# Block attention of a Perceiver layer: neighbours' tiles loaded by one repeating transfer, rotation on VectorE, sums over keys in halves

## The chip, the cores and the metric

The kernel runs on one core of a Trainium2 chip. The metric is the device time of one execution in microseconds. The kernel before took 2400.67 us (median of 3 runs, 2400.48 to 2401.24).

## The reference

x is (16, 64, 256), that is 1024 rows of 256; the context ctx_2048 is (16, 1601, 256). The layer adds three blocks to x, each on a layer-normalised x:

1. Cross attention with weights and activations rounded to 8 bits: self-attention over the 64 rows of a sequence, and attention of the 64 rows over the 1601 context rows (16 heads of 128 in 8 groups of keys), then a projection. It is nearly all of the work.
2. Block attention with ternary weights, the block that the change touches:

```python
qkv = bitlinear(rmsnorm(x, attn_norm_w), qkv_w).reshape(B, S, 3, NH, HD)   # 16 heads of 16
q = apply_rope(q, cos, sin)
k = apply_rope(k, cos, sin)
qb, kb, vb = (blk(q), blk(k), blk(v))        # blocks of bt = S // 8 = 8 rows
scores = jnp.einsum('bnhqd,bnhkd->bnhqk', qb, kb) * HD ** (-0.5)
scores = jnp.where(causal, jnp.finfo(scores.dtype).min, scores)
attn = jax.nn.softmax(scores, axis=-1)
ctx = jnp.einsum('bnhqk,bnhkd->bnhqd', attn, vb)
x1 = x + bitlinear(ctx, o_w)
hn = rmsnorm(x1, ffn_norm_w)
gate, val = jnp.split(hn @ ffn_up_w.T, 2, axis=-1)
return x1 + bitlinear(jax.nn.silu(gate) * val, ffn_down_w)
```

   Here x is (16, 64, 256), so S = 64: each row attends only to the rows of its own block of 8, up to itself. apply_rope turns each pair of halves (x1, x2) of a head into x1 cos - x2 sin, x2 cos + x1 sin. bitlinear rounds its input to 8 bits, row by row, by the row's largest absolute value, and multiplies by weights in -1, 0, 1.
3. A gated feed-forward network with ternary weights, 256 to 704 to 256, with scales by row.

## The kernel before

**Tiles and order.** The 1024 rows are NT = 8 tiles of 128 rows (two sequences each), which stay on the chip as xr[i]. The cross attention of a tile is cut into four units (half of the heads, one sequence), each of 13 chunks of 128 context rows; a step is one chunk, and a tile takes 52 steps. For each chunk a unit projects keys (ps_k, L624), stores them in DRAM (kd, L655), reads them back transposed (kT, L665), multiplies them with the queries (s, L696), and later, 18 to 20 steps on, subtracts the maximum (L754), takes the exponential (L758) and accumulates with the context rows ctxN (acc, L772). The 13 chunks of several units are in flight at once, so the engines always have the next chunk's work.

All parts of the kernel are written as Python generators, put into a heap with a step and a rank, with hand-written lists of the steps between the pieces (SCHEDULE, PACE). The heap gives one recorded order of instructions. The framework's scheduler then orders the instructions of each engine from that, and its pools give out the buffers, so a change in one place can move instructions of all engines. At run time each engine's queue, SP's and ACT's queues of transfers too, is worked off strictly in order. Transfers take eight semaphore lanes in turn, so that an issue may have to wait for the eighth before it.

**The changed part.** `last_parts(i, start)` (L990) does blocks 2 and 3 for tile i, spread over the steps of later tiles' cross attention. For the last tile nothing is left beside it except chunks of the feed-forward network of tiles 3 to 6 (LATE, L1209), which `fill(...)` places among its parts: `gated` (L1173: product pgu_late on TensorE, tanh on ACT, sg_late and hd_late on VectorE) and `down` (L1196: po_f, ot, output). Its steps:

- Normalise, quantise (`act_quant`, L961), multiply by the ternary weights: qk (128 rows x 512: 16 heads of 16 for q, then the same for k) and v (128 x 256).
- Rotate: GpSimd (POOL) writes r1 = qk times the cosines (L1018), VectorE writes r2 = the swapped halves times the sines in two instructions (L1024) and adds r2 to r1 (L1029).
- Store the rotated k and v in DRAM as kv, e = 0 for k and e = 1 for v, each as two halves a = 0, 1 of 8 heads, 128 rows x 128 (L1034).
- `near(e, a)` (L1037) loads, for every row, the 8 rows of its block side by side: a tile of 128 x 1024 floats in which row p holds the 8 x 128 values of block p // 8. That is the same 16 x 1024 floats eight times over. Eight transfers of 64 KB do it, the k-th one writing rows k, 8 + k, 16 + k and so on. They are issued on SP; for K of the last tile every other one goes on ACT's queue. So 32 transfers a tile: K a=0, K a=1, later V a=0, V a=1.
- `product(out, x, y, order)` (L1046) multiplies on VectorE over the whole 128 x 1024 (L1049) and sums by one reduction (L1050). For the scores it multiplies the row's q, repeated over 8 neighbours, with K and sums over the 16 channels. For the result cx it multiplies the softmax with V and sums over the 8 neighbours, for which the reduction reads with a stride.
- Mask, maximum, exponential and division between the two (L1065 to L1076).
- cx is quantised by `act_quant`: am (L965) is the row's largest absolute value, aq_q (L974) the rounded values, tr_aq their transposition on TensorE (L982); then po_o (L1093), xa, another norm, and the rest of the block.

`near` and `prod` tiles come from the pool wp (tag "w", 10 buffers), from which the weights' pieces (wproj, wup, w_ff, w_dn, tern_w) come as well. Tile i's last_parts run during the cross attention of tiles i+1 and i+2; those of the last one end the kernel.

Of the kernel before, what the change touches and what calls it, by code (L numbers as in the profile page):

```python
# [19 lines left out]
ALU = mybir.AluOpType  # L20
AX = mybir.AxisListType
PSUM = bass.MemoryType.PSUM

P = 128
# [49 lines left out]
def body(tc, ctx, a):  # L74
    nc = tc.nc
    V, A, PE, GP = nc.vector, nc.scalar, nc.tensor, nc.gpsimd
# [763 lines left out]
    def fill(where):  # L840
        n = FILL.get(where, 0)
        for fn in late[:n]:
            fn()
        del late[:n]
# [100 lines left out]
    def b2(name):  # L945
        return one.tile([P, 512], F32, tag="b2", name=name, bufs=3)

    def rmsnorm(src, wrow, name):
        sq = b1("sq3")
        ss = small.tile([P, 1], F32, tag="ss3", name="ss3")  # L950
        A.activation(sq, src, AF.Square, accum_out=ss)
        ms = small.tile([P, 1], F32, tag="ms1", name="ms1")
        V.tensor_scalar(ms, ss, 1.0 / H, EPS, ALU.mult, ALU.add)
        rs = small.tile([P, 1], F32, tag="rs1", name="rs1")
        GP.tensor_tensor(rs, ms, nhalf[:, 0:1], ALU.pow)
        yield 1
        h = b1(name)
        V.scalar_tensor_tensor(h, src, rs, wrow, ALU.mult, ALU.mult)
        return h
# [30 lines left out]
    def last_parts(i, start):  # L990
        need(8, "x", i)
        last = i == NT - 1
# [6 lines left out]
        h = yield from rmsnorm(xa, rows[:, 0, :], "h")  # L999
# [15 lines left out]
        if last:  # L1015
            fill("rope")
        r1, r2 = b2("r1"), b2("r2")
        GP.tensor_tensor(  # L1018
            r1.rearrange("p (h d) -> p h d", h=32), qk.rearrange("p (h d) -> p h d", h=32),
            rope[:, 0:16].unsqueeze(1).to_broadcast([P, 32, 16]), ALU.mult,  # L1020
        )
# [10 lines left out]
        kv = dram.tile([2, 2, P, P], F32, tag="kv3", name="kv3")  # L1032
# [3 lines left out]

        def near(e, a):  # L1037
            t = wp.tile([P, 1024], F32, tag="w", name="near")
            src = kv[e, a].rearrange("(n j) c -> n (j c)", j=8)
            for k in range(8):  # L1040

                q = nc.scalar if last and e == 0 and k % 2 else nc.sync
                q.dma_start(out=t.rearrange("(n t) x -> n t x", t=8)[:, k, :], in_=src)
            return t

        def product(out, x, y, order):  # L1046

            t = wp.tile([P, 1024], F32, tag="w", name="prod")
            V.tensor_tensor(t.rearrange("p (h j d) -> p h j d", h=8, j=8), x, y, ALU.mult)  # L1049
            V.reduce_sum(out, t.rearrange("p (h j d) -> p " + order, h=8, j=8), axis=AX.X)  # L1050

        near_k = [near(0, a) for a in range(2)]
        yield 2
        sc = one.tile([P, 16, 8], F32, tag="sc3", name="sc3")
        for a in range(2):
            if last:
                fill("sc%d" % a)
            product(
                sc[:, 8 * a : 8 * a + 8, :],
                r1[:, a * P : (a + 1) * P].rearrange("p (h d) -> p h d", h=8).unsqueeze(2).to_broadcast([P, 8, 8, 16]),  # L1060
                near_k[a].rearrange("p (j h d) -> p h j d", j=8, h=8), "h j d",
            )
            yield 1
        near_v = [near(1, a) for a in range(2)]
        V.tensor_tensor(sc, sc, cmask.unsqueeze(1).to_broadcast([P, 16, 8]), ALU.add)  # L1065
        mx = small.tile([P, 16], F32, tag="mx3", name="mx3", bufs=2)
# [11 lines left out]
        cx = one.tile([P, H], F32, tag="cx3", name="cx3")  # L1078
        for a in range(2):
            if last:  # L1080
                fill("av%d" % a)
            product(
                cx[:, a * P : (a + 1) * P].rearrange("p (h d) -> p h d", h=8),
                sc[:, 8 * a : 8 * a + 8, :].unsqueeze(3).to_broadcast([P, 8, 8, 16]),
                near_v[a].rearrange("p (j h d) -> p h j d", j=8, h=8), "h d j",
            )
            yield 1
        to = ternary_piece(1536, 512).rearrange("p (k o) -> p k o", k=2)
# [176 lines left out]
    for i in range(NT):  # L1265
        base = 52 * i
        for hh in range(2):
            for bb in range(2):
                unit(i, hh, bb, base + 26 * hh + 13 * bb)
            spawn(base + 26 * hh + 13 + 34 - 2 + (2, 1)[hh], 6.5, paced("pair", pair_out(i, hh, 4 if i < NT - 1 or hh == 0 else None)))  # L1270
        ln0, sa0, qx0 = SCHEDULE[i] if i in SCHEDULE else (
            base - 22, [base + o for o in (-15, 0, 8, 21)], [base + o for o in (-16, -7, 15, 18)]
        )
        spawn(ln0, 1.0, paced("ln" if i else "ln_first", ln_tile(i)))
        for p in range(4):
            spawn(sa0[p] - 2, 5.0, paced("sa", self_attention(i, p)))
            spawn(qx0[p] - 2, 3.0, paced("qx", queries(i, p)))
        l0 = base + {NT - 3: 95, NT - 2: 88, NT - 1: 82}.get(i, 90)
        spawn(l0, 4.5, paced("last" if i < NT - 1 else "last_tile", last_parts(i, l0)))
    spawn(-8, 1, bias_rows())  # L1280
    spawn(60, 5.7, ternary())
    order = [(kind, p) for p in range(4) for kind in ("wq", "wkv", "wqx", "wproj")]
# [76 lines left out]
```

## Time and profile before

| | us |
|---|---|
| median of 3 runs | 2400.67 (2400.48 to 2401.24) |
| the profiled execution | 2402.98 |
| its span, first to last instruction | 2400.8 |
| mean granted TensorE clock | 0.991 |
| ACT busy | 1667.5 |
| instructions in all | 40267 |
| transfers near<-kv | 248 on SP, 8 on ACT, 64 KB each |
| bytes moved | 485.17 MB, 202 GB/s on average |

The profile is of one execution. Engines are PE (TensorE), PEld (its weight loads), DVE (VectorE), ACT (ScalarE), POOL (GpSimd) and SP, and L12 is line 12 of the kernel. A row of a timeline has the start in us from the beginning of the span, the busy time, the engine and line, the operation, the output and inputs by the program's names, their shapes, how often it stands there in a row, and in brackets the idle time before it with what ended it. In rows of stretches come start:end, its length, the busy time of PE, PEld, DVE, ACT and POOL with the number of instructions, the granted clock, the share of the DMA engines' time and GB/s. In the line of 40 slices each digit is the busy share of 60 us in tenths.

For the changed lines the groups of the profile give: L1049 1.22 us, L1050 1.21 us for the scores and 1.86 to 1.93 for cx, L1029 0.69, L1018 (POOL) 1.27 to 1.51, L1024 0.41 to 1.50, one near issue on SP 0.587 in the median.

### The profile page before, as it was taken

To read this page: it belongs to the slowest core of one execution; us is meant where nothing else is said; L and a number is where in the kernel's file an instruction comes from. 1 tells how busy PE (TensorE), PEld (TensorE's weight loads), DVE (VectorE), ACT (ScalarE), POOL (GpSimd) and SP (SyncE) were. 2 spreads that over 40 slices of the span, in tenths; PEclk is the share of its full clock that TensorE was granted. 3 is DMA by queue.
4 is the path that set the end of the run, shared out by engine and by line. 5 is a ranking of instruction groups with operands and counts; after the bars stand their busy time and mean duration, and the time that the engine had idled before them with its cause. 6 is when DMAs were issued, how large, how long until landed. Compare 5 with 4: busy or idle time off the path is not lost.

```text
span 2400.8 us, 40267 instructions
## 1 busy us (share of the span) xinstructions
PE 2319.9 (97%) x12477; PEld 1761.5 (73%) x12477; DVE 1856.3 (77%) x4562; ACT 1667.5 (69%) x3744; POOL 798.4 (33%) x1016
## 2 busy tenths in 40 slices
PE   7999999999999999999999999999999999999995
PEld 4567777777777777877777777777777777677874
DVE  7577777878887788778887879777888777876766
ACT  4667777776876777767776777777677777776631
POOL 3333223333232433334333333324334343242200
PEclk9999999999999999999999999999999999999998
DMA  8889878876977779776987779877697776965323
GB/s 257 240 236 248 244 180 222 208 195 170 272 216 190 183 204 256 200 208 164 240 233 191 205 184 241 223 191 187 174 261 214 193 174 176 272 172 141 115 92 111
DMA packets 683661, 485.17 MB, mean 202 GB/s; under 512 B 464476, under 2 KB 592952, under 8 KB 683448
## 3 DMA queue, kind: packets, MB, share of 16 engines
q1 hardware_dynamic: 682904, 481.91, 75.4%
q8 instruction: 100, 1.64, 0.3%
q14 instruction: 113, 0.93, 0.1%
q10 hardware_dynamic: 544, 0.69, 0.1%
HBM read 271.03 MB, written 113.11 MB: 160 GB/s over the span
## 4 chain that ended last, share of the span: by engine, by line
PE 70%; DVE 11%; issue 5%; DMA 5%; ACT 4%; POOL 4%; SPq 1%; ACTq 0%; POOLq 0%; DVEq 0%
PE acc L772 22%; PE ps_k L624 21%; PE s L696 12%; PE po_x L863 2%; PE po_p L329 2%; ACT P L706 2%; PE ps_q L378 2%; POOL rsx L568 2%; POOL rs L223 1%; DMA kT<-kd 1%; DVE P L754 1%; PE sc L490 1%; PE pgu L1180 1%; PE tr_pc L799 1%; DVE M L715 1%
## 5 line engine op out<-in xcount | busy, mean ns | idle before, releaser
L772 PEld LDWEIGHTS acc<-ctxN,P 128*128 128x128 f32 (+1 forms) x4160 | 713.3, 191 | 212.3 <-issue 135.2
L772 PE MATMUL acc<-ctxN,P 128*128 128x257 f32 (+5 forms) x4160 | 799.8, 338 | 4.8 <-DMA ctxN<-in_ctx_n 2.7
L624 PE MATMUL ps_k<-wkx,ctxT 128*128 128x512 f32 x1600 | 760.2, 597 | 12.5 <-DVE wkx L1252 9.4
L706 ACT ACTIVATE P<-s,rsx 128x128 f32<-128x128 f32 x1536 | 439.4, 373 | 136.5 <-PE s L696 131.7
L567 POOL TENSOR_SCALAR vx<-ss 128x4 f32<-128x4 f32 x402 | 140.0, 348 | 1112.7 <-DVE ss L564 742.2
L568 POOL TENSOR_TENSOR rsx<-vx,nhalf 128x4 f32<-128x4 f32 x402 | 457.0, 1137 | 33.0
L624 PEld LDWEIGHTS ps_k<-wkx,ctxT 128*128 128x128 f32 x1600 | 278.1, 192 | 210.4 <-issue 189.9
L696 PE MATMUL s<-qx,kT 128*128 128x128 f32 x3072 | 412.1, 277 | 9.1 <-ACT qn L388 3.2
L696 PEld LDWEIGHTS s<-qx,kT 128*128 128x128 f32 x3072 | 377.6, 192 | 25.9 <-ACT qn L388 4.7
L715 DVE TENSOR_TENSOR M<-P,M 128x512 f32<-128x512 f32 (+1 forms) x384 | 263.6, 686 | 154.2 <-ACT P L706 138.3
L651 ACT COPY kh<-ps_k 128x1024 uint16<-128x1024 uint16 x360 | 366.6, 1018 | 4.9 <-DMA kd<-kh 4.9
L758 ACT ACTIVATE P<-P 128x512 f32<-128x512 f32 (+1 forms) x416 | 266.3, 641 | 141.4 <-DVE P L754 139.3
L559 ACT ACTIVATE sq<-ps_k 128x512 f32<-128x512 f32 x402 | 243.0, 604 | 167.8 <-PE ps_k L624 131.0
L564 DVE TENSOR_REDUCE ss<-sq 128x4 f32<-128x512 f32 x402 | 272.9, 679 | 27.2 <-ACT sq L559 27.0
L754 DVE TENSOR_TENSOR P<-P,mx 128x512 f32<-128x512 f32 (+1 forms) x416 | 284.0, 683 | 0.0
L223 POOL TENSOR_TENSOR rs<-ve,nhalf 128x4 f32<-128x4 f32 (+2 forms) x128 | 126.1, 986 | 287.6 <-DVE ve L222 267.8
L229 DVE TENSOR_SCALAR qn<-qn,mv,rs 128x128 f32<-128x128 f32 x256 | 76.8, 346 | 46.0 <-POOL rs L223 45.1
L219 DVE BATCH_NORM_STATS2 st<-qn 128x6 f32<-128x128 f32 x256 | 64.7, 273 | 23.4 <-ACT qn L388 23.4
L306 ACT CAST w_hi<-wproj 128x1024 fp32r<-128x1024 f32 x60 | 63.3, 1056 | 27.2 <-DMA wproj<-wproj 23.7
L307 DVE TENSOR_TENSOR wproj<-wproj,w_hi 128x1024 fp32r<-128x1024 f32 x60 | 73.0, 1219 | 9.4 <-ACT w_hi L306 8.7
L417 POOL TENSOR_TENSOR q_y<-qn,brow 128x512 f32<-128x512 f32 x32 | 51.8, 1619 | 53.4 <-DVE qn L229 45.9
L329 PE MATMUL po_p<-wproj,cat 128*128 128x256 f32 x272 | 67.0, 293 | 0.0
(233 smaller groups left out, 2817.9 us busy)
## 6 DMA issues: line engine op xcount, KB each, us to landing
kd<-kh SPq DMA_DIRECT2D x375, 256.0 KB
ctxT<-in_ctx SPq DMA_DIRECT2D x192, 256.0 KB
ctxN<-in_ctx_n SPq DMA_DIRECT2D x384, 128.0 KB
wproj<-wproj SPq DMA_DIRECT2D x68, 512.0 KB
wq<-wq SPq DMA_DIRECT2D x32, 512.0 KB
wkv<-wkv SPq DMA_DIRECT2D x32, 512.0 KB
wqx<-wqx SPq DMA_DIRECT2D x32, 512.0 KB
near<-kv SPq DMA_DIRECT2D x248, 64.0 KB
```

Source lines behind the costliest of these rows:

```text
L223: GP.tensor_tensor(rs[:, :g], ve[:, :g], nhalf[:, :g], ALU.pow)
L559: A.activation(sq[:n], ps[:n], AF.Square)
L564: ordered("dve", V.reduce_sum(ss[:n], sq[:n].rearrange("p (g d) -> p g d", g=4), axis=AX.X))
L568: ordered("pool", GP.tensor_tensor(rs[:n], ve[:n], nhalf[:n, 0:4], ALU.pow))
L624: PE.matmul(ps[:n, :], lhsT=st["cxT"][c // 2][:, k, o : o + n], rhs=wkx[:, k, 512 * hh : 512 * (hh + 1)], start=k == 0, stop=k == 1,)
L651: A.copy(t, src.bitcast(U16).rearrange("p (c e) -> p e c", e=2))
L696: PE.matmul(ps[:n, g * P : (g + 1) * P], lhsT=kT[:, g, 0:n], rhs=qxs[i, hh][:, bb, 2 * g : 2 * g + 2, :].rearrange("p h s -> p (h s)"), st ...
L706: A.activation(pc[:, g * P : (g + 1) * P], ps[:, g * P : (g + 1) * P], AF.Copy, scale=rs[:, g : g + 1])
L715: ordered("dve", V.tensor_tensor(st["M"][:n], pc[:n], st["M"][:n], ALU.max))
L754: ordered("dve", V.tensor_tensor(pc[:n], pc[:n], st["mx"][:n].rearrange("p g q -> p (g q)"), ALU.add))
L758: A.activation(pc[:n], pc[:n], AF.Exp)
L772: m = PE.matmul(ps, lhsT=pc[:n, g * P : (g + 1) * P], rhs=cx[:n, o : o + w], start=g < 3 and c == 0, stop=c == NC - 1, skip_group_check=g ...
```

## The change

Three edits, all in `last_parts`. The cosine product of the rotation is computed on VectorE instead of GpSimd. `near` issues one transfer of 512 KB per tile, whose source repeats each block's 1024 floats eight times (a stride of zero in the middle of 16 x 8 x 1024), all on SP but K a=1 of the last tile, which goes on ACT. `product` returns the products; the scores are reduced as before, and cx is summed by three additions in place: 8 neighbours to 4 (512 values of each row), 4 to 2 (256), 2 to 1 (128).

```diff
         r1, r2 = b2("r1"), b2("r2")
-        GP.tensor_tensor(
+        V.tensor_tensor(
             r1.rearrange("p (h d) -> p h d", h=32), qk.rearrange("p (h d) -> p h d", h=32),
             rope[:, 0:16].unsqueeze(1).to_broadcast([P, 32, 16]), ALU.mult,
         )
...
         def near(e, a):
             t = wp.tile([P, 1024], F32, tag="w", name="near")
-            src = kv[e, a].rearrange("(n j) c -> n (j c)", j=8)
-            for k in range(8):
-
-                q = nc.scalar if last and e == 0 and k % 2 else nc.sync
-                q.dma_start(out=t.rearrange("(n t) x -> n t x", t=8)[:, k, :], in_=src)
+            q = nc.scalar if last and e == 0 and a else nc.sync
+            q.dma_start(
+                out=t, in_=kv[e, a].rearrange("(n j) c -> n (j c)", j=8).unsqueeze(1).to_broadcast([16, 8, 1024])
+            )
             return t
 
-        def product(out, x, y, order):
+        def product(x, y):
 
             t = wp.tile([P, 1024], F32, tag="w", name="prod")
             V.tensor_tensor(t.rearrange("p (h j d) -> p h j d", h=8, j=8), x, y, ALU.mult)
-            V.reduce_sum(out, t.rearrange("p (h j d) -> p " + order, h=8, j=8), axis=AX.X)
+            return t
...
-            product(
-                sc[:, 8 * a : 8 * a + 8, :],
+            t = product(
                 r1[:, a * P : (a + 1) * P].rearrange("p (h d) -> p h d", h=8).unsqueeze(2).to_broadcast([P, 8, 8, 16]),
-                near_k[a].rearrange("p (j h d) -> p h j d", j=8, h=8), "h j d",
+                near_k[a].rearrange("p (j h d) -> p h j d", j=8, h=8),
+            )
+            V.reduce_sum(
+                sc[:, 8 * a : 8 * a + 8, :], t.rearrange("p (h j d) -> p h j d", h=8, j=8), axis=AX.X
             )
...
-            product(
-                cx[:, a * P : (a + 1) * P].rearrange("p (h d) -> p h d", h=8),
+            t = product(
                 sc[:, 8 * a : 8 * a + 8, :].unsqueeze(3).to_broadcast([P, 8, 8, 16]),
-                near_v[a].rearrange("p (j h d) -> p h j d", j=8, h=8), "h d j",
+                near_v[a].rearrange("p (j h d) -> p h j d", j=8, h=8),
+            ).rearrange("p (h x) -> p h x", h=8)
+            for n in (64, 32):
+                V.tensor_tensor(t[:, :, 0:n], t[:, :, 0:n], t[:, :, n : 2 * n], ALU.add)
+            V.tensor_tensor(
+                cx[:, a * P : (a + 1) * P].rearrange("p (h d) -> p h d", h=8), t[:, :, 0:16], t[:, :, 16:32], ALU.add
             )
```

## The prediction

> **What bounds the kernel now.** I read the busy shares and slices first, then busy time by stretch, then the timelines of the queues in the stretches that lose time.
>
> ```profile
> PE 2319.9 (97%) x12477; PEld 1761.5 (73%) x12477; DVE 1856.3 (77%) x4562; ACT 1667.5 (69%) x3744; POOL 798.4 (33%) x1016
> PE   7999999999999999999999999999999999999995
> PEclk9999999999999999999999999999999999999998
> ```
>
> TensorE is the bound: busy for 2319.9 of 2400.8 us at nearly full clock. No VectorE instruction saved in the middle is worth its own length; only idle time of PE can be won. The changed code runs once for each of eight tiles of rows, the first about 500 us in, the last in the final 55 us. The second view is busy time by stretch (start:end, length, then PE).
>
> ```profile
> 580.00:605.00 25.00, 23.36 (x129) 18.14 (x129) 21.89 (x50) 17.01 (x38) 9.63 (x11) 1.00 0.69 174
> 1153.00:1178.00 25.00, 24.34 (x130) 18.27 (x129) 22.68 (x52) 17.59 (x37) 9.61 (x11) 1.00 0.77 189
> 2025.00:2060.00 35.00, 32.60 (x161) 22.48 (x160) 30.09 (x72) 24.72 (x55) 10.14 (x13) 1.00 0.89 226
> 2270.00:2290.00 20.00, 15.21 (x82) 12.84 (x81) 18.01 (x39) 9.81 (x19) 0.93 (x1) 0.91 0.62 201
> 2340.00:2370.00 30.00, 11.99 (x54) 7.99 (x51) 21.94 (x40) 3.60 (x8) 1.51 (x1) 0.73 0.50 147
> ```
>
> The first three are what follows the loading of V's neighbours in three tiles: PE misses 1.64, 0.66 and 2.40 us. The stretches 867:892, 1438:1463 and 1718:1743 miss 0.97, 1.27 and 1.29 (24.03, 23.73, 23.71 of 25), so the six make 8.2 us. Quiet ones lose nothing (1000:1025 and K's 823:848 have 25.00 of 25). All of 520:2270 has 1729.67 of 1750: 20.3 idle. 2270:2290 loses 4.8, and 2340:2370 loses 18, which is the tail: the last tile's chain with too little else to do.
>
> Why PE misses time after V's transfers is in SP's timeline and in PE's rows just behind it:
>
> ```profile
> 1153.12 9.96 SPq L1043 DMA_DIRECT2D near<-kv  x16
> 1163.13 0.58 SPq L688 DMA_DIRECT2D qb<-qbd  x1
> 1163.81 1.68 SPq L665 DMA_TRANSPOSE kT<-kd  x1
> 599.96 0.46 PE L772 MATMUL acc<-ctxN,P 128*128 128x257 f32 x1 [1.38 <-DMA ctxN<-in_ctx_n]
> 1173.35 0.46 PE L696 MATMUL s<-qx,kT 128*128 128x128 f32 x2 [0.29 <-DMA kT<-kd]
> ```
>
> Sixteen issues hold SP for 10 us (0.6 each); the loads behind them (kT, ctxN) are late for PE some 10 us on. The tail is read on VectorE, SP, ACT and PE:
>
> ```profile
> 2342.47 1.84 DVE L1024 TENSOR_TENSOR r<-qk,shp 128x256 f32<-128x256 f32 x2 [0.66 <-ACT qk L1006]
> 2347.01 15.19 SPq L1043 DMA_DIRECT2D near<-kv  x24
> 2346.98 5.44 ACTq L1043 DMA_DIRECT2D near<-kv  x8
> 2351.61 1.23 DVE L1049 TENSOR_TENSOR prod<-r,near 128x1024 f32<-128x1024 f32 x1 [4.82 <-DMA near<-kv]
> 2361.95 1.86 DVE L1050 TENSOR_REDUCE cx<-prod 128x128 f32<-128x1024 f32 x1
> 2364.30 1.23 DVE L1049 TENSOR_TENSOR prod<-sc,near 128x1024 f32<-128x1024 f32 x1 [0.49 <-DMA out<-ot]
> 2367.45 0.42 DVE L965 TENSOR_REDUCE am<-cx 128x1 f32<-128x256 f32 x1
> 2369.55 0.39 PE L982 MATMUL tr_aq<-identb,aq_q 128*128 128x128 bf16 x2 [13.13 <-DVE aq_q L974]
> ```
>
> VectorE waits 4.8 us for K's neighbours, then works through to am at 2367.45, and PE waits 13.1 us for that. What moves am moves the end.
>
> **Tail, part by part.** *Rotation.* Beside POOL's product VectorE's two take 1.84 us. On VectorE alone: one 128x512 and two 128x256 products, which follow one another at 0.61 and 0.34 (intervals of such rows): 1.29 plus the interleaved late chunk. The sum of r1 starts some 0.3 us earlier (0 to 0.6), and with it the store of r.
> *K.* Before, the first of two K tiles lands at 2351.61, 4.6 us after its first issue. After: two transfers of 512 KB, on SP and ACT, issued about 2346.7; first packets 0.9 to 1.0 later, as now; 1 MB at 290 to 366 GB/s (366 is what the queue moved at 2366–2372; now it moves 105 to 172 here) is 2.9 to 3.6 us; 0.5 to the wake-up. Both land at about 2351.1 (2349.7 to 2352.6). SP then issues the late output row and both V; another 1 MB behind K, at 2351 + 3.6, is there at about 2355, and is needed only after two K products, two sums and the softmax (4.9 + 2.3), at 2358. ACT is no longer held for 5.44 us, so the late chunks' tanh, which came 7.4 us late at 2352.47, moves into the wait for K.
> *VectorE's chain.* From the first product to am it takes 15.84 us now. Out of it go: late chunks at 2354.01–2355.46, 1.45 (into K's wait); two ot rows, 0.66; the wait for V, 0.49; two cx sums of 1.89, replaced by adds on 512, 256 and 128 elements, 0.72 + 0.46 + 0.32 = 1.50 when each waits for the one before, so 0.78. Left: 12.5 (11.6 if other work fills the gaps between dependent ones, by intervals 0.61, 0.34, 0.21; 12.7 with all steps dependent). am then comes at 2351.1 + 12.5 = 2363.6 rather than 2367.45: **3.9 us** (2352.6 + 12.7 gives 2.1; 2349.7 + 11.6 gives 6.2). Behind am nothing changes, PE's clock is at 0.50 there already, and wup, issued at 2363.34 now, is issued earlier, since SP loses 28 issues.
>
> **Body.** *SP.* Per tile 32 issues become 4: 28 x 0.6 = 17 us of SP time gone. K's were spread over 25 us at no loss; V's cost the 8.2 us above. In tile seven, 2270:2290 loses 4.8: PE waits 4.06 at 2284.94 for an aq_q whose am is at 2280.40 behind the second cx at 2277.98; in the changed order of VectorE this cx comes some 20 instructions earlier. At best 8.2 + 4.8 = 13.0; at worst nothing is won and the new order loses as much elsewhere. The changed order of instructions differs from about 500 us on, on every engine (PE differs in 7115 lines), and the 25 us idle in 520:2290 is an average of what such orders lose. I take half: **6.5**.
> *VectorE.* Per tile 0.95 (the rotation row of 1.37 against 0.42 beside POOL) goes and 0.61 comes; sums save 0.8 to 1.5. Hidden: 77% busy, and PE is the bound. If that cover were gone, 1.5 x 7 = 10 us more gain.
> *New waits on VectorE.* Between the rotation's last sum and the first K product stand 23 VectorE instructions rather than 52 in tiles one to five, 14 and 7 in tiles six and seven; by their row lengths 11.9 us (26.7 before), 7.5 and 4.5. K needs, from tile three's rows (sum 1103.10, store 1104.49, first near 1108.69) and a landing of 5.84 us as for a 512 KB wproj in the chain of waits: 11.4 us, or 9 if SP comes sooner. Tiles one to five are covered (VectorE is not always busy, so 11.9 lasts 13 or so); tiles six and seven may stop VectorE for 2 and 4 us. Queued behind are P and M products that PE needs; PE can run on for about as long. I take **-1** (0 to -6).
> *POOL.* One instruction of 1.27 to 1.5 us a tile goes; POOL is at 33%, worth 0.
>
> **A rule against it.** The trace first: VectorE's second rotation row takes 1.37 us while POOL's L1018 runs and 0.42 otherwise, but P's products (L754, two operands in SBUF, mean 684 ns) and M's (686 ns) show no lengthening although POOL runs its small power (L568, 1.04 us x402) a third of the time. The Trainium skill, page "SBUF — State Buffer", section "Who interferes with whom", says that a VectorE instruction with two SBUF inputs and a GpSimd one reading SBUF exclude each other, and that reductions do not contend. By it the adds in halves are exposed where the sums were not: 48 adds at a third of the time by half of 1.04 is 8 us of VectorE; by the rows 0. The measured rows decide; in the tail POOL has no row from 2344 to 2372.
>
> **Sum.** 3.9 + 6.5 - 1 = 9.4. The profiled execution took 2402.98 us (span 2400.8), 2.3 above the median of the runs, 2400.67; the difference goes on the median: **2391.3 us**.
>
> **Rivals.** *Only the tail* (0.16): the new order loses as much as SP wins; for it: the idle 8.2 is what one fixed order leaves late, and another order can be late at another load; against: quiet stretches lose nothing. 2400.67 - 3.9 = 2396.8.
> *SP parked on V* (0.15, the slower side): V a=1 waits in each of tiles one to six for a buffer that VectorE frees, directly behind V a=0, and the next in SP's queue is the transpose of kT that PE reads. In the changed order K's second product stands 15 us of VectorE work behind the first, and V close to it. For a hold of W us, by the rate above (10 us cost 1.4): -3.9 - 8.2 + 6 x (1.4 + W - 10); it decides from W = 10.6, and W = 14 gives 2400.67 + 20 = 2421. Against: before, V's first issue waits for VectorE too, and SP reached it without pause at 1153.12.
> *The repeat isn't spread* (0.04): if one DMA engine carried a whole transfer, 128 rows x 0.2 us (4 KB packets take 0.17 to 0.27) = 26 us; K and V in the tail would cost about 40 and tiles more: 2440 and above. Against: its destination is 128 rows and each row one 4 KB run, as now.
> *No change* (0.03): order and tail cancel, 2400.
>
> **How the numbers follow.** Likeliest case 0.62, own range 2381.5 (6.2 + 13.0) to 2397. What is no change for this kernel: within 0.2%, 4.8 us. Only-the-tail (2.1 to 6.2) is faster by more in about 0.06 of its 0.16, else the same. Faster 0.68, same 0.13, slower 0.19. The range 2381.5 to 2401 holds the first two cases and no change; the slower ones are left out.
>
> **What would show it.** SP: four near issues a tile of about 0.6 us, none followed by a pause in SP above 10 us before the next kT. PE: the six stretches after V at most 0.5 us idle each, tile seven's wait for tr_aq under 2 us. Tail: K landing near 2351 less the body's gain, am 12.5 us after the first product, adds at 0.69, 0.42 and 0.28. Wrong if a K landing takes over 8 us, VectorE waits for near in tiles one to five, or the cx adds are slower than 1.9 us together.

## The result and the profile after

The changed kernel takes 2409.28 us (median of 10 runs, 2405.61 to 2416.88), the kernel before beside it 2400.95 (2396.88 to 2404.91). The ratio is 1.0037, 95% interval 1.0027 to 1.0048: slower by some 9 us, where 9.4 us less was forecast. The profiled execution has a span of 2408.0 us.

The tail did what was forecast, nearly. From the last tile's qk on ACT (L1006; 2341.75 before, 2352.19 after) to the end of the span it takes 55.8 us instead of 59.05. So 3.2 us are won there, and the body before it ends 10.4 us later. Busy time by stretch of the changed kernel shows where (PE is the column after the length, the last three are granted clock, DMA share and GB/s):

```profile
580.00:600.00 20.00, 16.00 (x76) 12.10 (x75) 11.28 (x32) 10.26 (x22) 6.41 (x9) 0.83 0.87 242
872.00:892.00 20.00, 16.09 (x93) 12.31 (x92) 11.82 (x31) 12.86 (x26) 7.14 (x11) 1.00 0.99 276
1160.00:1180.00 20.00, 15.33 (x79) 12.27 (x78) 11.56 (x33) 10.27 (x20) 6.54 (x10) 0.83 0.91 266
2270.00:2290.00 20.00, 20.00 (x135) 17.72 (x134) 11.18 (x20) 12.01 (x30) 2.66 (x4) 1.00 0.26 83
520.00:2270.00 1750.00, 1716.29 (x9346) 1316.90 (x9353) 1367.84 (x3360) 1274.14 (x2850) 584.37 (x750) 0.99 0.77 202
```

Tile seven's stretch, which lost 4.8 us before, loses nothing. But 520:2270 has 33.7 us without PE instead of 20.3, and 23.0 of them lie in six stretches of 20 us, one behind each of tiles one to six: the three shown and 1450:1470, 1735:1755 and 2015:2035 (15.20, 16.76 and 17.59 busy). Outside the six, 10.7 us are idle: the places that lost time before have been emptied (the 145 us behind V's issues of tiles one to six have PE busy for 144.03), and one new place has been opened in each of these tiles.

What happens there is in the chain of waits of tile three (start, duration, what) and in the view of who waited for whom (total, times, longest):

```profile
1164.97 0.46 SPq L255
...
1166.40 5.56 DMA wq<-wq
...
1171.99 1.05 ACT w_hi L306
...
1173.07 0.04 DVE wq L307
...
1174.21 0.69 DVE red L723
...
1175.04 0.37 PE tr_r L438
```

```profile
ACT w_hi L306 <- DMA wq<-wq: 19.5, 11, 3.4
DVE wq L307 <- ACT w_hi L306: 20.9, 9, 4.0
PE tr_r L438 <- DVE red L723: 21.1, 7, 4.8
```

wq is a piece of self-attention's weights (512 KB, L298), of another part of the kernel. It is loaded into the same pool wp as near and prod. ACT casts it to w_hi (L306), VectorE subtracts that from it (L307). red is a maximum over keys that VectorE takes for the cross attention (L723), and tr_r its transposition on TensorE (L438). In the changed kernel SP issues the second wq piece of a tile at 1166.40, behind the two wup loads (L255), and it lands 5.56 us later; ACT comes to the cast 3.0 us before that and holds everything behind it; VectorE is held at L307, its reduction red (L723) behind that is late, and PE waits 4.67 us at tr_r. None of these instructions is in the diff. The issue, the cast and tr_r in the timelines of the changed kernel:

```profile
1166.40 0.38 SPq L298 DMA_DIRECT2D wq<-wq  x1
1171.99 1.04 ACT L306 CAST w_hi<-wq 128x1024 fp32r<-128x1024 f32 x1 [3.00 <-DMA wq<-wq]
1175.04 0.37 PE L438 MATMUL tr_r<-ident,red 128*4 128x128 f32 x1 [4.67 <-DVE red L723]
```

In the kernel before the same wq is cast 7.0 us behind its issue, with no wait, and the view of waits has only the third of these rows:

```profile
1183.23 0.69 SPq L298 DMA_DIRECT2D wq<-wq  x1
1190.23 1.04 ACT L306 CAST w_hi<-wq 128x1024 fp32r<-128x1024 f32 x1
PE tr_r L438 <- DVE red L723: 0.3, 1, 0.3
```

It is the same in the other tiles. ACT comes to the cast of the second wq piece 7.0 to 7.8 us behind its issue in tiles one to five of the kernel before (3.4 in tile six, with a wait of 0.55); in tiles one to six of the changed kernel it comes 2.1 to 4.5 us behind it, and can begin after 5.4 to 7.3.

The tail after, in the timelines of SP, ACT, VectorE and PE:

```profile
2357.22 0.53 SPq L1040 DMA_DIRECT2D near<-kv  x1
2357.15 0.61 ACTq L1040 DMA_DIRECT2D near<-kv  x1
2361.85 1.23 DVE L1048 TENSOR_TENSOR prod<-r,near 128x1024 f32<-128x1024 f32 x1 [1.42 <-DMA near<-kv]
2364.13 1.23 DVE L1048 TENSOR_TENSOR prod<-r,near 128x1024 f32<-128x1024 f32 x1 [1.06 <-DMA near<-kv]
2374.57 0.42 DVE L965 TENSOR_REDUCE am<-cx 128x1 f32<-128x256 f32 x1
2376.66 0.40 PE L982 MATMUL tr_aq<-identb,aq_q 128*128 128x128 bf16 x2 [17.75 <-DVE aq_q L974]
```

From qk to am it is 22.38 us (2352.19 to 2374.57), 25.70 before.

### The profile page after: what moved, and what is told of

It reads as the page before. It is cut to its first block, busy times and chain, and to the rows that moved or that the text cites. A ratio compares the mean times of both kernels' runs of the same rounds, so it can differ in the third digit from the quotient of the medians.

```text
span 2408.0 us, 39988 instructions
## 1 busy us (share of the span) xinstructions
PE 2317.4 (96%) x12469; PEld 1765.0 (73%) x12477; DVE 1838.5 (76%) x4602; ACT 1669.1 (69%) x3744; POOL 771.0 (32%) x1008
## 4 chain that ended last, share of the span: by engine, by line
PE 66%; DVE 14%; issue 7%; DMA 5%; POOL 5%; ACT 3%; SPq 0%; POOLq 0%; ACTq 0%; DVEq 0%
PE acc L772 21%; PE ps_k L624 19%; PE s L696 11%; POOL rsx L568 2%; PE po_p L329 2%; PE po_x L863 2%; DMA wq<-wq 2%; POOL rs L223 2%; PE ps_q L378 1%; DVE P L754 1%; DVE M L715 1%; ACT P L706 1%; DVE st L219 1%; DVE qn L229 1%; DMA wproj<-wproj 1%
## 5 line engine op out<-in xcount | busy, mean ns | idle before, releaser
L624 PE MATMUL ps_k<-wkx,ctxT 128*128 128x512 f32 x1600 | 761.6, 598 | 14.4 <-DVE wkx L1257 9.3
L568 POOL TENSOR_TENSOR rsx<-vx,nhalf 128x4 f32<-128x4 f32 x402 | 440.3, 1095 | 33.1
L307 DVE TENSOR_TENSOR wproj<-wproj,w_hi 128x1024 fp32r<-128x1024 f32 x60 | 72.8, 1215 | 9.2 <-ACT w_hi L306 9.2
L306 ACT CAST w_hi<-wproj 128x1024 fp32r<-128x1024 f32 x60 | 63.5, 1061 | 17.7 <-DMA wproj<-wproj 12.5
L329 PE MATMUL po_p<-w_hi,cat 128*128 128x256 f32 x240 | 65.6, 307 | 2.3 <-DVE cat L316 1.4
```

Source lines behind the costliest of these rows:

```text
L329: PE.matmul(po[:, 0:H], lhsT=cat[:, h, :], rhs=w[:, h * H : (h + 1) * H], start=h + e == 0, stop=h == 3 and e == len(ws) - 1,)
L568: ordered("pool", GP.tensor_tensor(rs[:n], ve[:n], nhalf[:n, 0:4], ALU.pow))
L624: PE.matmul(ps[:n, :], lhsT=st["cxT"][c // 2][:, k, o : o + n], rhs=wkx[:, k, 512 * hh : 512 * (hh + 1)], start=k == 0, stop=k == 1,)
```

## The experiments

Each ratio is against the kernel before on the same chip, with its 95% interval; medians of different calls are not compared, since before itself had medians of 2401 to 2406.

**Which edit moves the time.** tr_alone is the kernel before with this alone:

```diff
-            src = kv[e, a].rearrange("(n j) c -> n (j c)", j=8)
-            for k in range(8):
-                q = nc.scalar if last and e == 0 and k % 2 else nc.sync
-                q.dma_start(out=t.rearrange("(n t) x -> n t x", t=8)[:, k, :], in_=src)
+            q = nc.scalar if last and e == 0 and a else nc.sync
+            q.dma_start(out=t, in_=kv[e, a].rearrange("(n j) c -> n (j c)", j=8).unsqueeze(1).to_broadcast([16, 8, 1024]))
```

> The kernel before with the transfer edit alone (near as one repeating transfer; rotation and sums as before). Order theory (this edit alone moves the second wq piece of each tile: its load and, on ACT, its cast come earlier, the cast a chunk's step closer to its load, and ACT, VectorE and PE wait for the landing): as slow as the change, 2407 to 2413 us, with idle stretches of 3 to 5 us before PE's tr_r once in each of tiles one to six. VectorE theory (the adds and the rotation on VectorE cost the time): 2390 to 2398, no such stretches. Contention theory (transfers of 512 KB crowd the queue): slow as well, but with the landings of all loads longer than before.

ve_alone is the changed kernel with the removed lines put back.

> The changed kernel with the eight transfers of before (rotation on VectorE and sums in halves stay). Order theory: the position of the wq casts is that of before, so 2396 to 2400 us: the tail's 0.3 and 0.8 to 1.5 and little else. VectorE theory: 2405 to 2412, slower than before. Contention theory: as before, 2396 to 2401.

Measured: tr_alone 1.0076 (1.0060 to 1.0092), ve_alone 0.9997 (0.9987 to 1.0006). The transfers alone cost more than the whole change, and more than the order theory had for them, with 36.7 us of ACT's waiting for wq; the VectorE edits without them are no change. This pair does not exclude contention.

**Taking the wait away.** load_early records the wq load two steps sooner and leaves the rest of self-attention in its steps:

```diff
-            spawn(sa0[p] - 2, 5.0, paced("sa", self_attention(i, p)))
+            spawn(sa0[p] - 4, 5.0, paced("sa", self_attention(i, p)))
-    "sa": [0, 0, 0, ...
+    "sa": [2, 0, 0, ...
```

> The changed kernel with the wq loads of self-attention recorded two steps earlier, the rest of its steps where they were: the load of the second piece then stands two chunks earlier on SP, its cast where it is in the changed kernel. Order theory: the six waits of ACT for wq (1.6 to 3.4 us) and the PE losses around them (7.1, 4.1, 7.0, 6.9, 3.4, 2.8 us, the lower granted clock after the longest among them; 31 in sum) go: 2378 us if nothing takes their place, 2394 if half is lost elsewhere. VectorE and contention theories: within 4 us of 2409.

Measured: 0.9952 (0.9936 to 0.9969), 2393.86 us, faster than both kernels. SP now issues wq ahead of wup, and ACT finds it there:

```profile
1147.78 0.32 SPq L298 DMA_DIRECT2D wq<-wq  x1
1154.01 0.40 SPq L255 DMA_DIRECT2D wup<-in_ffn_up_w  x1
1156.57 1.04 ACT L306 CAST w_hi<-wq 128x1024 fp32r<-128x1024 f32 x1
```

The cast comes 8.8 us behind the issue and waits for nothing; PE's waits for red at tr_r are 0.5 us in sum. The edit leaves the transfers of the change, their number and their size as they are, so these alone don't make the loss. Against the change's 1.0037 this is 0.85%, some 20 us of the 31 that the expectation counted, for an edit that touches no line of the diff. The control is the same edit in the kernel before:

> The kernel before with the wq loads recorded two steps earlier, as in load_early: the control. Order theory: before has only 3.4 us of ACT's waiting for wq to lose, and its idle behind V's transfers stays, so 2397 to 2403 us. If an earlier wq load is worth 15 us by itself, whatever the transfers: 2385 to 2391.

It gives 0.9986 (0.9975 to 0.9998), 1.4 permille. So of the 20 us some 3 may be had without the change; the other 17 are had only where the change has made its wait.

**Delaying the cast instead.** cast_late has "sa": [3, -1, 0, ...] in the changed kernel.

> The changed kernel with the pieces after the wq load of self-attention recorded three steps later (and one less afterwards), so that the cast of the second wq piece stands one chunk later and its load one chunk later too; the number and size of transfers and their burst with wup, wkv and tern_w stay. Order theory: the waits of ACT for wq shrink by up to a chunk (5.5 us), so 2380 to 2398. Contention theory: the loads land as late as now and something else waits for them, within 4 us of 2409. VectorE theory: within 4 us of 2409.

Measured: 1.0102 (1.0082 to 1.0123), outside every expectation. ACT's waits for wq did fall to 3.3 us, but the rest of self-attention runs two steps later, wkv's cast now waits 12.1 us, and PE's waits for red at tr_r are 13.5 us in nine pieces. From 500 us to the last tile's qk PE is idle for 51.8 us, 35.3 in the change and 26.1 before. The edit moved more than it was meant to, and decides nothing about the size of the wait for wq.

**Distance or crowding.** wup_late records the two wup loads behind the norm that follows them:

```diff
-        w_up = [piece("wup", ...) for k in range(2)]
         yield 1
         hn = yield from rmsnorm(xa, rows[:, 1, :], "hn")
+        w_up = [piece("wup", ...) for k in range(2)]
```

> The changed kernel with the two wup loads recorded behind the norm that follows them instead of ahead of it: the second wq piece is issued ahead of wup rather than behind it; its cast moves with it and stays one chunk closer than before. If wq lands late because two wup transfers of 512 KB stand ahead of it (SP reaches it late and the queue is full): the waits for wq fall from 19.5 us in sum to under 8 and the time to 0.995 to 1.000 of before. If only the distance between load and cast counts: waits as in the change, 1.002 to 1.006.

Measured: 1.0064 (1.0042 to 1.0085). wq is issued ahead of wup and is still late, because its cast was placed sooner as well:

```profile
1158.68 0.41 SPq L298 DMA_DIRECT2D wq<-wq  x1
...
1162.32 0.46 SPq L298 DMA_DIRECT2D wkv<-wkv  x1
...
1163.01 1.04 ACT L306 CAST w_hi<-wq 128x1024 fp32r<-128x1024 f32 x1 [1.94 <-DMA wq<-wq]
...
1167.94 1.05 ACT L306 CAST w_hi<-wkv 128x1024 fp32r<-128x1024 f32 x1 [2.76 <-DMA wkv<-wkv]
```

It lands 4.3 us after its issue, where behind wup it took 5.56. In tiles one to five the cast can begin 4.2 to 4.9 us behind the issue (5.4 to 7.3 in the change, behind wup), so the two wup loads do delay wq, by one to two us. But ACT comes to the cast 1.2 to 2.4 us behind the issue: even the sooner landing is too late for that, and well within the 7.0 to 7.8 us that five tiles of the kernel before had. The distance between load and cast decides, and crowding is a part of what it has to cover. ACT's waits for wkv's load, 12.2 us in sum, are new in this kernel; the change has none.

**Which transfers.** k_one has one transfer for K and eight for V, v_one the reverse, both with the VectorE edits:

```diff
+            if e == 0:    # v_one: e == 1
+                q = ...
+                q.dma_start(out=t, in_=src.unsqueeze(1).to_broadcast([16, 8, 1024]))
+                return t
             for k in range(8):
```

> The changed kernel with one transfer for K's neighbours only; V's come by eight. The second wq piece then stands on SP and its cast on ACT as in the kernel before, a chunk further apart than in the change. Order theory: no waits above 2 us for wq, no 3 to 5 us stretches before tr_r; the 8.2 us behind V's issues stay, the tail keeps most of its 3.3: 0.996 to 0.9995 of before. If a repeating transfer is slow by itself, wherever it is: 1.002 or more.

> The changed kernel with one transfer for V's neighbours only; K's come by eight. The second wq piece and its cast then stand a chunk closer, as in the change. Order theory: the waits for wq and the stretches before tr_r are back, 1.002 to 1.008 of before. If a repeating transfer is slow by itself: between k_one and the change.

Measured: k_one 0.9936 (0.9912 to 0.9961), v_one 0.9951 (0.9936 to 0.9966). For v_one I had counted chunks in the order of instructions and taken a distance of less than one for a wait; the trace has wq issued at 1178.39 and cast at 1184.80, 6.4 us apart, and 1.3 us of waiting in all. Counting was too coarse by a few us, and the time went with the wait, not with the count. Each half is a gain of about half a per cent or more; only both together lose. k_one came out better than its expectation (0.996 to 0.9995), which had the idle behind V's issues stay. It shows that the eight issues for V need not hurt: in its order they hold SP no longer in one block of 10 us but over 22 us, and PE has 23.00 of 23:

```profile
1127.70 1.15 SPq L1046 DMA_DIRECT2D near<-kv  x2
...
1132.68 0.48 SPq L1046 DMA_DIRECT2D near<-kv  x1
...
1143.84 5.53 SPq L1046 DMA_DIRECT2D near<-kv  x9
```

k_alone is the kernel before with one transfer for K and nothing else:

> The kernel before with one thing changed: K's neighbours by one transfer (V by eight, rotation and sums as before). In its order the second wq piece and its cast stand as in k_one. Order theory: waits for wq stay under 6 us in sum, V's issues are spread, and the two VectorE edits of k_one are worth little beside PE: 0.993 to 0.997 of before. If the VectorE edits carry k_one's gain, as the rotation did beside both transfers: 0.998 to 1.002.

It gives 0.9948 (0.9931 to 0.9964): most of k_one's gain is in this one edit.

**The VectorE edits beside both transfers.**

> The changed kernel with the cosine product of the rotation back on GpSimd. The transfer edit alone is 15 us slower than the whole change, so one of the two VectorE edits takes back 15 us of its loss. If it is the sums in halves (they end V's use of buffers 1.5 us sooner per tile, so wup, tern_w and wq behind it get buffers and are issued sooner): 2407 to 2413 us here, the waits for wq on ACT near 20 us in sum. If it is the rotation: 2418 to 2426, waits near 37.

> The changed kernel with both sums by one reduction each, as before. If the sums in halves take back the 15 us: 2418 to 2426 us, the waits of ACT for wq near 37 us. If the rotation does: 2407 to 2413, near 20.

Measured: rope_back 1.0078 (1.0057 to 1.0099), halves_back 1.0047 (1.0030 to 1.0064). The expectation left open which of the two; by the times it is the rotation that takes back what the change has better than tr_alone. ACT's wait for wq does not rank these: 23.7 us in rope_back, 34.9 in halves_back. PE's own waits at tr_r and tr_m are close together (25.4 and 22.7; the change 23.3). The profiled executions of rope_back and the change are 13.1 us apart (spans of 2421.1 and 2408.0): 2.1 in the tail, 5.5 more idle time of PE between 500 us and the tail (40.8 against 35.3), and 5.6 more busy time of PE there, at a mean granted clock of 0.987 against 0.989 over the execution. What in rope_back's order makes these stays open.

**The tail by itself.** last_only makes the whole change in the last tile alone (`last` selects the engine, the transfers and the sums).

> The whole change in the last tile alone: the seven others load by eight transfers, rotate on both engines and sum by reduction, with the order of before up to there. Tail term of the forecast (3.9, by the changed kernel's trace 3.25 from qk on ACT to the end): 2396 to 2399 us, 0.9982 to 0.999 of before. If the tail's gain is only the body's, moved: within 1 us of before.

It gives 0.9984 (0.9970 to 0.9997), 0.7 to 7 us less: the tail's gain is its own.

All kernels together. The first column is PE's waits in the profiled execution at tr_r for red (L723) and at tr_m for M (L727), the second when ACT comes to the cast of the second wq piece, behind the issue of its load, in tiles one to six (below zero: ahead of the issue):

| kernel | PE's waits there, us | ACT at the cast, us | ratio to before |
|---|---|---|---|
| before | 0.3 | 3.4 to 7.8 | 1 |
| the change | 23.3 | 2.1 to 4.5 | 1.0037 |
| tr_alone | 24.7 | -1.6 to 0.9 | 1.0076 |
| rope_back | 25.4 | 1.0 to 4.5 | 1.0078 |
| halves_back | 22.7 | -0.8 to 1.6 | 1.0047 |
| wup_late | 29.4 | 1.2 to 2.4 | 1.0064 |
| cast_late | 15.1 | 8.8 to 10.7 | 1.0102 |
| ve_alone | 0.3 | 3.5 to 7.7 | 0.9997 |
| last_only | 0.3 | 3.4 to 8.2 | 0.9984 |
| before_load_early | 1.4 | 15.6 to 20.7 | 0.9986 |
| load_early | 5.3 | 7.6 to 8.8 | 0.9952 |
| v_one | 1.6 | 6.4 to 9.5 | 0.9951 |
| k_alone | 1.0 | 8.8 to 9.4 | 0.9948 |
| k_one | 1.0 | 8.8 to 9.4 | 0.9936 |

No kernel above 6 us in the first column is faster than before, and none under 6 is slower. Among the slower ones the column does not rank: cast_late, with the smallest wait of them and ACT at the cast only after 8.8 us and more, is the slowest; its other waits are told above.

## Why the prediction was wrong

- *Bound and reading of the profile.* Right. PE's idle time was what counted, and the idle behind V's issues and in tile seven (13.0 us) is what the change emptied: 10.7 us of idle are left in 520:2270 outside the six new places, against 20.3 before, and 2270:2290 is full. load_early, the change without its new wait, gives 0.9952; the forecast of 2391.3 was 0.9961. That these two agree is in part luck: in load_early's profiled execution (2397.35 us, the slowest of its seven) PE's idle time from 500 us to the last tile's qk is 25.6 us, 26.1 before, since small waits stand in other places (4.8 us at tr_m), so the 6.5 us of idle time were not won as forecast there. k_one shows that they could be: 16.4 us by the same measure.
- *Tail, 3.9 us.* Right mechanism, measured 3.2 to 3.3. VectorE could begin on K a=0 4.63 us after its issue and on K a=1 6.98, where 4.4 was taken for both (the forecast's own terms add up to 4.3 to 5.1). All three terms were too low. The first packet came 1.3 us behind the issue, as in the kernel before, where 0.9 to 1.0 had been read. From 2358.5 to 2363.2, first packet to last, 1.14 MB moved at 244 GB/s, other transfers among it, not at 290 to 366. And 0.9 us lay between a tile's last packet and its product, not 0.5. From the first product to am it took 12.72 us, 1.06 of them the wait for K a=1, where 12.5 stood.
- *VectorE.* Rows as forecast (groups of the changed kernel):

```profile
L1088 DVE TENSOR_TENSOR prod<-prod 128x512 f32<-128x512 f32 x16 | 10.8, 681 | 0.0
L1088 DVE TENSOR_TENSOR prod<-prod 128x256 f32<-128x256 f32 x16 | 6.6, 417 | 0.0
L1024 DVE TENSOR_TENSOR r<-qk,shp 128x256 f32<-128x256 f32 x16 | 6.4, 416 | 0.0
L1018 DVE TENSOR_TENSOR r<-qk,shp 128x512 f32<-128x512 f32 x8 | 5.5, 690 | 7.3 <-ACT qk L1006 7.3
L1089 DVE TENSOR_TENSOR cx<-prod 128x128 f32<-128x128 f32 x16 | 4.4, 282 | 0.0
```

  Hidden, as said: ve_alone is no change. The rule of the Trainium skill, "SBUF — State Buffer", section "Who interferes with whom", would have lengthened the adds. 39 of the 48 had a POOL instruction run beside them and are no longer for it: 0.681 us in the mean for the 14 of 128x512 beside one, 0.682 for the two without. With POOL's big product the trace agrees with the page: the rotation's own 0.84 (mean before) fell to 0.42 when that product went. The rows were the better guide for POOL's short instructions. (Those of L568 fill 19% of the span before, 402 of 1.14 us in the mean; the prediction had 1.04 us and a third of the time, which is POOL's whole busy share.)
- *New waits on VectorE, -1.* Wrong place. VectorE waited for near only in the last tile (2.5 us); the 2 and 4 us feared for tiles six and seven did not come.
- *Body, +6.5: the step that failed.* "At worst nothing is won and the new order loses as much elsewhere" was no bound. The body was to end 5.5 us sooner (6.5 less the 1 for VectorE) and ended 10.4 later. The new order won about what was to be had and lost 23 us of PE's time elsewhere, at one instruction per tile: tr_r in tiles one to five, tr_m in tile six. I looked for new waits on what the change moves (near, kv, wup), not on what shares its pool and its queue. The order of the changed kernel showed it: before, 95 stores of keys stand ahead of the load of tile one's second wq piece on SP and 94 copies of keys from ps_k ahead of its cast on ACT; after, 91 and 89. The load moved four chunks up and the cast five.
- *Rivals.* SP was not parked on V: both issues take 1.20 us at 1139.84 and the next kT follows at 1142.51. The repeat is spread; a 512 KB tile lands in 4.6 us, not 26. The slower side was right to be there, with the wrong mechanism.

What the runs don't settle is why the scheduler draws the cast too close to its load only when both K and V come by one transfer.

## What to carry to other kernels

Where a scheduler and a shared pool decide the order, the cost of an edit is not in the edited lines: list every load that shares its pool or queue, and compare the distance from each load to its first consumer in the two orders, in microseconds of the trace. A load needs its landing time (here 5.4 to 7.3 us for 512 KB in the change, from 4.2 with less ahead of it) ahead of an in-order consumer. One that missed it by 1.6 to 3.4 us held three engines and cost 23.0 us of PE's time in six tiles; the change had freed 14.4 (9.6 in 520:2270 outside the new places, 4.8 in tile seven). And try the halves of an edit separately: here each half gains 0.5% and both together lose 0.4%.

## What the runs showed of the hardware

**A pause of PE costs more than its length.** Stretches of the changed kernel around the pause in tile three (4.67 us) and in tile two (3.91 us); the third column from the end is the granted clock:

```profile
1170.00:1175.00 5.00, 0.37 (x2) 0.00 (x0) 1.94 (x3) 3.01 (x7) 0.38 (x1) 0.78 1.12 334
1175.00:1178.00 3.00, 2.96 (x13) 2.81 (x14) 1.42 (x3) 1.33 (x3) 1.27 (x2) 0.50 0.84 266
1178.00:1182.00 4.00, 4.00 (x16) 2.96 (x16) 1.04 (x2) 2.44 (x7) 0.00 (x0) 0.80 0.34 84
...
885.00:888.00 3.00, 3.00 (x21) 2.50 (x20) 1.05 (x2) 2.39 (x7) 1.27 (x2) 1.00 1.06 331
```

The same six matmuls behind the one and behind the other:

```profile
1175.20 1.92 PE L772 MATMUL acc<-ctxN,P 128*128 128x257 f32 x6
884.77 1.04 PE L772 MATMUL acc<-ctxN,P 128*128 128x257 f32 x6
```

After 4.67 us the clock is at half for 3 us with PE busy, and the 0.80 of the next 4 us makes it some 1.6 more; after 3.91 us it stayed at full. In tr_alone it was at 0.50 behind a pause of 2.67 us (1177:1179). The Trainium skill, "TensorE: Matmul & The Clock Gate", section "What's actually happening", has a window of about 3.4 us that runs freely; that fits the outcomes here, half clock after 2.67 and 4.67 us and full clock after 3.91.

**Two large transfers on two queues were served one after the other.** K's two tiles of the last tile were issued at 2357.15 (ACT) and 2357.22 (SP). In 2357.5:2360.4 124 packets of SP's queue and 5 of ACT's moved; in 2360.4:2362.8 128 of ACT's and 39 of SP's. So the second product began 2.3 us behind the first, 1.06 of it in waiting. In nine other kernels that load K's two tiles this way it is 2.1 to 2.4 us. Before, with eight transfers of 64 KB on each queue, both moved side by side: in 2348.2:2350 95 packets of SP's and 76 of ACT's, in 2350:2352 91 and 90.
